# Plain loads in order of need, a first projection by quarters and biases spread by DMA, at the start of a GRU and mixture-of-experts kernel

## The chip, the cores and the metric

The kernel runs on one core of one Trainium2 chip. The metric is the device time of an execution in microseconds; before and after are compared as medians of several runs. Beside the runs there is one profiled execution, from which every duration below is taken.

## The reference

`x` is [8, 256, 512]: 8 sequences of T = 256 steps, the inputs of the GRU; `cond` [8, 512] is its state at the start. A GRU runs over the steps, a mixture of experts with a shared expert follows, and `x` is added.

```python
def cell(h, x):
    gi = x @ W_ih + b_ih          # [512] x [512, 1536]
    gh = h @ W_hh + b_hh
    i_r, i_z, i_n = split(gi, 3); h_r, h_z, h_n = split(gh, 3)
    r = sigmoid(i_r + h_r); z = sigmoid(i_z + h_z)
    n = tanh(i_n + r * h_n)
    h_new = (1 - z) * n + z * h
# over the rows of all h: router, softmax, top 2 of 8 experts, weights normed to 1
out = x + sum_e combine[e] * (silu(g_e) * u_e) @ w_down[e] + (silu(g_s) * u_s) @ w_sh_down
```

All data are float32.

## The kernel before

The time axis is cut into 16 blocks of 16 steps. A block is 8 x 16 = 128 tokens, so one block fills the partitions. For each block the kernel projects `x` with `W_ih` (`project`, TensorE through `multiply`, L310), adds the biases into `gi` (VectorE, L356), and stores `gi` to a DRAM tile (L366 for r and z, L368 for n). From there `load_seeds` (L386) fetches the gate inputs of four steps at a time in the layout of a step, since the tokens' partitions are not those of the step; `turn_seeds` (L391) transposes the n part. A `step` has 48 matmuls (L419) for the gates r, n and z: 16 each, four column groups of the array by four quarters of the state. Before them ScalarE copies the gate inputs into the banks (`open_gate`, L403); afterwards VectorE transposes each bank (L430), and sigmoid, tanh and three more vector operations make the next state (L438 to L455). GpSimd keeps a copy of the states (L458).

Between the steps TensorE is fed with pieces of other work in an order written out by hand: the projections of later blocks, the shared expert (L707), the router. A quota spreads these pieces over the blocks. After the last step come the rest of the shared expert and 35 tiles of routed tokens (L661, L788).

The state's 512 features lie on 128 partitions and 4 quarters q. Before the change feature d = j x 128 + q x 32 + i lies on partition 32 j + i in quarter q. So each weight matrix is loaded by `by_state` in transfers to 32 partitions (L142 for `W_ih`, L152 for `W_hh`, 12 transfers of 256 KB each), and a block of `x` is loaded in 8 transfers to 16 partitions (L119) and transposed in 32 by 32 blocks by VectorE (`transpose_x`, L299). The weights of the GRU lie in the space of the last four experts, which are loaded when the GRU no longer needs it.

The order at the start sets what this text is about. SP issues half of `x_0` (ScalarE's queue the other half and both biases, each to one partition, and the start state), then `W_ih`, `x_1`, `W_hh`, and, from `transpose_x(0)`, `x_2`; only then stand the stores of block 0 and its seed loads. The biases are spread over the partitions by three matmuls with a row of ones (`spread_bias`, L259) and copied by ScalarE (L260), between the third and the fourth quarter of each gate's projection. Before the first step stand `transpose_x(1)` and four pieces of block 1's projection.

The two hardware DMA queues (SP's and ScalarE's) share eight completion semaphores; in the program as built, a transfer first waits until the earlier transfer with the same semaphore has landed.

Of the kernel before, what the change touches and what calls it, by code (L numbers as in the profile page):

```python
# [9 lines left out]
F32 = mybir.dt.float32  # L10
BF16 = mybir.dt.bfloat16
I32 = mybir.dt.int32
AF = mybir.ActivationFunctionType
ALU = mybir.AluOpType
# [3 lines left out]
P = 128  # L18
TS = 16
# [6 lines left out]
def kernel(  # L26
# [48 lines left out]

    nc = tc.nc
    B, T, D = x.shape
    G3 = w_ih.shape[1]  # L80
# [27 lines left out]
    x_tiles = {}  # L108
    NG = 4

    def by_turns(t_, k):

        v = t_.rearrange("(g c) t (j m) -> j c t g m", c=2, j=4)[:, :, k * TS : (k + 1) * TS]
        return [(slice(32 * j + TS * c, 32 * j + TS * (c + 1)), v[j, c]) for j in range(4) for c in range(2)]

    def load_x(k, queues=(nc.sync,)):
        xt = xpool.tile([P, NG, P], F32, tag="x", name=f"x_{k}")
        for i, (ps, src) in enumerate(by_turns(x, k)):
            queues[i % len(queues)].dma_start(xt[ps], src)  # L119
        x_tiles[k] = xt  # L120

    def by_state(w):
# [1 line left out]
        v = w.rearrange("(j q i) n -> j i q n", j=4, i=32)  # L124
        return [(slice(32 * j, 32 * j + 32), v[j]) for j in range(4)]

    load_x(0, (nc.sync, nc.scalar))


    we = wts.tile([P, E, NW, D], F32, name="we")  # L130
    wih = we[:, E - 2 : E].rearrange("p e w n -> p (e w n)").rearrange("p (q n) -> p q n", q=NQ)
    whh = we[:, E - 4 : E - 2].rearrange("p e w n -> p (e w n)").rearrange("p (q n) -> p q n", q=NQ)

    bias = const.tile([P, G3], F32, name="bias")
    bias_row = we[0:1, 0, 0:3].rearrange("p w n -> p (w n)")
    bias_h = we[0:1, 0, 3:5].rearrange("p w n -> p (w n)")
    nc.scalar.dma_start(bias_row, b_ih.unsqueeze(0))
    nc.scalar.dma_start(bias_h, b_hh[0 : 2 * D].unsqueeze(0))
    for g in range(3):
        cols = slice(g * D, (g + 1) * D)  # L140
        for ps, src in by_state(w_ih[:, cols]):
            nc.sync.dma_start(wih[ps, :, cols], src)  # L142
    h = state.tile([P, NQ, 32], F32, name="h")
    nc.vector.memset(h, 0.0)
    h0v = h0.rearrange("b (j q i) -> b j q i", q=NQ, j=4)
    for j in range(4):
        nc.scalar.dma_start(h[32 * j : 32 * j + B], h0v[:, j])
    load_x(1)
    for g in (0, 2, 1):
        cols = slice(g * D, (g + 1) * D)  # L150
        for ps, src in by_state(w_hh[:, cols]):
            nc.sync.dma_start(whh[ps, :, cols], src)  # L152
    wg = wts.tile([P, NQ, 32], F32, name="wg")
    nc.vector.memset(wg, 0.0)
    wsu = [wts.tile([P, NQ, 2, IM], F32, name=f"wsu_{c}") for c in range(NSH)]
# [11 lines left out]
        loads.append(issue)  # L167

    def load_shared():
        load(*((wg[ps, :, 0:E], src) for ps, src in by_state(w_gate)))  # L170
        up = w_sh_gate_up.rearrange("d (two c f) -> two c d f", two=2, f=IM)
        down = w_sh_down.rearrange("(c f p) n -> c p f n", p=P, f=NF)
        for c in range(NSH):
            for two_i in range(2):
                parts = [(wsu[c][ps, :, two_i, :], src) for ps, src in by_state(up[two_i, c])]
                load(*parts[:2])
                load(*parts[2:])
            for f in range(NF):
                load((wsd[c][:, f, :], down[c][:, f, :]))

    def load_expert(e):
        for q in range(NQ):
            load((we[:, e, q, :], w_gate_up[e, q * P : (q + 1) * P, :]))
        for f in range(NF):
            load((we[:, e, NQ + f, :], w_down[e, f * P : (f + 1) * P, :]))


    ident = const.tile([P, P], F32, name="ident")
    make_identity(nc, ident)
    seeds = [const.tile([P, SC, 2 * P], F32, name=f"seeds_{i}") for i in range(NS)]  # L190
    seeds_n = const.tile([P, SC, P], F32, name="seeds_n")
    seed_hn = const.tile([P, P], F32, name="seed_hn")
    states = [const.tile([P, NQ, 32], F32, name=f"hT_{i}") for i in range(NH)]
    for st in [*seeds, seeds_n, seed_hn, *states]:
        nc.vector.memset(st, 0.0)

    tri = const.tile([P, P], BF16, name="tri")
# [51 lines left out]
        ]  # L249
        for i in range(NB)  # L250
    ]
    nc.vector.tensor_tensor(bias_row[:, 0 : 2 * D], bias_row[:, 0 : 2 * D], bias_h, ALU.add)
    one = we[0:1, 2, 0, 0:P]
    nc.vector.memset(one, 1.0)

    def spread_bias(g):
        ps = ps_mm.tile([P, D], F32, tag="mm", name=f"biasp_{g}")
        cols = slice(g * D, (g + 1) * D)
        nc.tensor.matmul(ps, one, bias_row[:, cols], start=True, stop=True)  # L259
        nc.scalar.copy(bias[:, cols], ps)  # L260

    b_hn = b_hh[2 * D : G3].rearrange("(j m) -> j m", j=4)
    for j in range(4):
        nc.gpsimd.dma_start(seed_hn[32 * j : 32 * j + B], b_hn[j].partition_broadcast(B))


    rows = dram.tile([B, T, D], F32, name="rows")
# [5 lines left out]
    nc.vector.tensor_copy(vacant[:, :, 0], lanes)  # L273
    load((listed[0 : E * NM], vacant), (listed[E * NM : E * NM + 1], vacant[0:1]))

    banks = {g: ps_gru.tile([P, D], F32, name=f"ps_{g}") for g in "rnz"}
    for bank in banks.values():  # L280
        nc.tensor.matmul(
            bank[:, 0:P], seeds[0][:, 0, 0:P], seeds[0][:, 0, 0:P], start=True, stop=True
        )


    xT_of = {}

    spare = deque()

# [7 lines left out]
    def transpose_x(k):  # L297
        xT = two.tile([P, NG, NQ, 32], F32, tag="xrT", name=f"xT_{k}")
        nc.vector.transpose(  # L299
            xT.rearrange("p g q s -> p (g q s)"), x_tiles.pop(k).rearrange("p g m -> p (g m)")  # L300
        )
        xT_of[k] = xT
        if k + 2 < NB:
            load_x(k + 2)

    def multiply(ps, lhs, rhs, start, stop):

# [32 lines left out]
    def project(k, g):  # L340

        box = {}

        def issue(q, cols):
            if q == 0 and cols.start == 0:
                box["ps"] = ps_mm.tile([P, D], F32, tag="mm", name=f"gip_{k}_{g}")
            multiply(
                box["ps"][:, cols],
                lambda c: xT_of[k][:, c, q, :],
                wih[:, q, g * D + cols.start : g * D + cols.stop],  # L350
                start=(q == 0 and cols.start == 0),
                stop=(q == NQ - 1 and cols.stop == D),
            )

        def end():
            nc.vector.tensor_tensor(  # L356
                gi[:, :, g, :],
                box["ps"].rearrange("p (j m) -> p j m", j=4),
                bias[:, g * D : (g + 1) * D].rearrange("p (j m) -> p j m", j=4),
                ALU.add,  # L360
            )
            if g > 0:
                to = gi_dram[k][g % 2].rearrange("j b t n -> (b t) j n")
                projected.add((k, "rzn"[g]))
                if g == 1:
                    nc.sync.dma_start(to.rearrange("p j (a n) -> p j a n", a=2), gi[:, :, 0:2, :])  # L366
                else:
                    nc.sync.dma_start(to, gi[:, :, 2, :])  # L368

        return [  # L370
            matmul_piece(lambda cols, q=q: issue(q, cols), end if q == NQ - 1 else None)
            for q in range(NQ)
        ]
# [4 lines left out]
    def load_seeds(c, of="nz"):  # L378

        k, o = divmod(c * SC, TS)  # L380
        steps = slice(o, o + SC)
        for g in of:
            assert (k, g) in projected
            tile_, src = (seeds_n, gi_dram[k][0]) if g == "n" else (seeds[c % NS], gi_dram[k][1])
            for j in range(4):
                nc.sync.dma_start(tile_[32 * j : 32 * j + B], src[j, :, steps, :])  # L386

    def turn_seeds(c):

# [12 lines left out]
        src = {"r": seeds[c % NS][:, t, 0:P], "z": seeds[c % NS][:, t, P : 2 * P], "n": seed_hn}  # L402
        nc.scalar.copy(banks[g][:, 0:P], src[g])  # L403

    whh_v = whh.rearrange("p q (a j m) -> p q a j m", a=3, j=4)
    hc_of = {}

    def hc_of_block(k):
# [2 lines left out]
    def step(n):  # L411
# [3 lines left out]
        for g, bank in banks.items():  # L415
            a = "rzn".index(g)
            for q in range(NQ):
                for j in range(4):
                    nc.tensor.matmul(  # L419
                        bank[32 * j : 32 * j + B, 0:P],  # L420
                        hT[:, q, 0:B],
                        whh_v[:, q, a, j, :],
                        start=False,
                        stop=(q == NQ - 1),
                        skip_group_check=True,
                    )
# [143 lines left out]
    def send_rows(k):  # L570

        hr = two.tile([P, NG, P], F32, tag="y", name=f"hr_{k}")
        nc.vector.transpose(
            hr.rearrange("p g m -> p (g m)"), hc_of_block(k).rearrange("p g q s -> p (g q s)")
        )
        for ps, dst in by_turns(rows, k):
            nc.sync.dma_start(dst, hr[ps])

    laid = {}

# [259 lines left out]
        under_way.update(up=stages, turn=last)  # L840


    transpose_x(0)
    nc.vector.transpose(states[0].rearrange("p q b -> p (q b)"), h.rearrange("p q i -> p (q i)"))
    for g in range(3):
        pieces = project(0, g)
        for piece in pieces[:-1]:
            piece[1]()
        spread_bias(g)
        pieces[-1][1]()  # L850
        if g > 0:
            load_seeds(0, "nzn"[g])
    turn_seeds(0)
    load_seeds(1)
    load_shared()

    projections = deque()
    projections.append((0, lambda: transpose_x(1)))
    for k in range(1, NB):
        for g in range(3):  # L860
            projections.extend(project(k, g))
            if g == 1 and k + 1 < NB:
                projections.append((0, lambda k=k: transpose_x(k + 1)))

    for _ in range(1 + NQ):
        projections.popleft()[1]()
    for g in banks:
        open_gate(0, g)
    for k in range(NB):
# [138 lines left out]
```

## Time and profile before

| | us |
|---|---|
| median of 3 runs | 1495.91 (1495.86 to 1499.71) |
| profiled execution | 1485.87 |
| its span | 1484.1 |
| TensorE matmuls busy | 1411.5 (95%) |
| VectorE busy | 744.3 (50%) |
| ScalarE busy | 418.2 (28%) |
| first projection starts | 11.0 |
| first step's matmuls start | 54.8 |

The page cuts the span into 40 slices of 37.1 us; TensorE's busy share in tenths and the rate of all transfers in the first five slices are 4, 6, 9, 9, 9 and 188, 80, 114, 118, 99 GB/s. In lines of the profile, L followed by a number is a line of the kernel, "<-" leads from an output to its inputs or from a waiting instruction to what ended its wait, SPq and ACTq are the queues of DMA issues of those engines, PE is TensorE, DVE VectorE, ACT ScalarE and POOL GpSimd. A float32 matmul appears as two records on PE.

### The profile page before, as it was taken

To read this page: it belongs to the slowest core of one execution; us is meant where nothing else is said; L and a number is where in the kernel's file an instruction comes from. 1 tells how busy PE (TensorE), PEld (TensorE's weight loads), DVE (VectorE), ACT (ScalarE), POOL (GpSimd) and SP (SyncE) were. 2 spreads that over 40 slices of the span, in tenths; PEclk is the share of its full clock that TensorE was granted. 3 is DMA by queue.
4 is the path that set the end of the run, shared out by engine and by line. 5 is a ranking of instruction groups with operands and counts; after the bars stand their busy time and mean duration, and the time that the engine had idled before them with its cause. 6 is when DMAs were issued, how large, how long until landed. Compare 5 with 4: busy or idle time off the path is not lost.

```text
span 1484.1 us, 75080 instructions
## 1 busy us (share of the span) xinstructions
PE 1411.5 (95%) x33082; PEld 1029.6 (69%) x33082; DVE 744.3 (50%) x2772; ACT 418.2 (28%) x1774; POOL 248.0 (17%) x497
## 2 busy tenths in 40 slices
PE   4699999999999999999999999999999999999995
PEld 1487777777777777877777777787777774444442
DVE  2356555556565556565646565656565643222221
ACT  0133232323333333333333333333333320222221
POOL 1122311111101010100001010101010212344442
PEclk8799999999999999999999999999999999999998
DMA  9244522222312011111011111111011323455453
GB/s 188 80 114 118 99 55 65 59 65 66 71 43 50 15 50 29 36 37 42 17 47 35 30 40 31 29 36 43 14 45 28 94 70 111 86 87 96 88 87 49
DMA packets 69226, 90.68 MB, mean 61 GB/s; under 512 B 13410, under 2 KB 46242, under 8 KB 68900
## 3 DMA queue, kind: packets, MB, share of 16 engines
q1 hardware_dynamic: 53056, 48.14, 12.6%
q0 software_dynamic: 15456, 37.57, 12.5%
q8 instruction: 261, 4.28, 1.2%
q14 instruction: 65, 0.53, 0.1%
q10 hardware_dynamic: 388, 0.16, 0.0%
HBM read 55.50 MB, written 30.32 MB: 58 GB/s over the span
## 4 chain that ended last, share of the span: by engine, by line
PE 90%; DMA 3%; DVE 3%; issue 2%; ACT 1%; SPq 0%; POOL 0%; DVEq 0%; ACTq 0%; POOLq 0%
PE ps_r L419 16%; PE gu_s L707 15%; PE ps_n L419 15%; PE ps_z L419 15%; PE gip L310 9%; PE gu_t L661 8%; PE po L310 7%; PE yp L788 4%; DMA we<-in_L_cond_W_hh_dram 1%; DMA we<-in_L_cond_W_ih_dram 1%; DVE zT L430 1%; DVE hn L454 0%; ACT z L449 0%; DVE hT L455 0%; PE ps_z L768 0%
## 5 line engine op out<-in xcount | busy, mean ns | idle before, releaser
L419 PEld LDWEIGHTS ps_r<-we,hT 128*8 128x8 f32 x8192 | 222.4, 89 | 120.8 <-ACT ps_z L403 72.0
L419 PE MATMUL ps_r<-we,hT 128*8 128x128 f32 x8192 | 278.3, 273 | 17.6 <-DVE hT L455 10.3
L419 PE MATMUL ps_z<-we,hT 128*8 128x128 f32 x8192 | 279.3, 273 | 3.2 <-issue 3.2
L419 PE MATMUL ps_n<-we,hT 128*8 128x128 f32 x8192 | 277.9, 273 | 0.0
L707 PE MATMUL gu_s<-hc,wsu 128*32 128x256 f32 x4096 | 247.2, 379 | 2.1 <-issue 2.1
L458 POOL COPY hc<-hT 128x32 f32<-128x32 f32 x256 | 62.7, 245 | 1045.8 <-DVE hT L455 1045.8
L419 PEld LDWEIGHTS ps_z<-we,hT 128*8 128x8 f32 x8192 | 229.8, 90 | 4.7 <-issue 4.3
L419 PEld LDWEIGHTS ps_n<-we,hT 128*8 128x8 f32 x8192 | 229.8, 90 | 0.2
L310 PE MATMUL gip<-we,xT 128*32 128x512 f32 (+1 forms) x1976 | 197.0, 506 | 29.9 <-DVE xT L299 22.5
L438 ACT ACTIVATE r<-rT 128x32 f32<-128x32 f32 x256 | 58.5, 229 | 508.5 <-DVE rT L430 506.3
L707 PEld LDWEIGHTS gu_s<-hc,wsu 128*32 128x32 f32 x4096 | 140.3, 110 | 84.8 <-issue 16.1
L430 DVE STREAM_TRANSPOSE rT<-ps_r 128x128 f32<-128x128 f32 x256 | 80.3, 314 | 179.3 <-PE ps_r L419 178.5
L430 DVE STREAM_TRANSPOSE nT<-ps_n 128x128 f32<-128x128 f32 x256 | 80.9, 316 | 127.4 <-PE ps_n L419 127.3
L310 PE MATMUL po<-wsd,act_s 128*32 128x256 f32 (+1 forms) x1408 | 134.2, 476 | 0.0
L661 PE MATMUL gu_t<-we,xrT 128*128 x280 | 131.7, 593 | 0.2 <-ACT xrT L770 0.2
L310 PEld LDWEIGHTS gip<-we,xT 128*32 128x32 f32 x1976 | 71.0, 111 | 85.1 <-issue 66.5
L403 ACT COPY ps_n<-seed_hn 128x128 f32<-128x128 f32 x256 | 68.8, 269 | 88.0 <-DVE nT L430 85.6
L430 DVE STREAM_TRANSPOSE zT<-ps_z 128x128 f32<-128x128 f32 x256 | 81.0, 316 | 13.6 <-PE ps_z L419 5.4
L446 ACT ACTIVATE nn<-nt 128x32 f32<-128x32 f32 x256 | 58.8, 230 | 81.6 <-DVE nt L444 81.4
L652 DVE TENSOR_TENSOR act_t<-gu_t,act_t 128x256 f32<-128x256 f32 x35 | 14.9, 424 | 131.4 <-ACT act_t L651 131.4
L794 POOL DMA_INDIRECT out_dram<-y,row x35 | 55.5, 1585 | 113.2 <-DVE y L791 95.9
L403 ACT COPY ps_r<-seeds 128x128 f32<-128x128 f32 x256 | 67.0, 262 | 18.8 <-DMA seeds<-gid_rz 18.6
(162 smaller groups left out, 1146.5 us busy)
## 6 DMA issues: line engine op xcount, KB each, us to landing
gid_rz<-gi SPq DMA_DIRECT2D x16, 512.0 KB
seeds<-gid_rz SPq DMA_DIRECT2D x256, 32.0 KB
we<-in_L_ffn_w_gate_up_dram POOLq DMA_DIRECT2D x32, 256.0 KB, 3.9
gid_n<-gi SPq DMA_DIRECT2D x16, 256.0 KB
seeds_n<-gid_n SPq DMA_DIRECT2D x256, 16.0 KB
wsu<-_L_ffn_w_sh_gate_up_dram POOLq DMA_DIRECT2D x32, 128.0 KB, 3.5
rows<-hr SPq DMA_DIRECT2D x128, 32.0 KB
we<-in_L_ffn_w_down_dram POOLq DMA_DIRECT2D x16, 256.0 KB, 4.0
```

Source lines behind the costliest of these rows:

```text
L310: nc.tensor.matmul(ps[32 * c : 32 * c + 32], lhs(c), rhs, start=start, stop=stop, skip_group_check=True,)
L403: nc.scalar.copy(banks[g][:, 0:P], src[g])
L419: nc.tensor.matmul(bank[32 * j : 32 * j + B, 0:P], hT[:, q, 0:B], whh_v[:, q, a, j, :], start=False, stop=(q == NQ - 1), skip_group_check= ...
L430: nc.vector.transpose(gT.rearrange("p a b -> p (a b)"), banks[g][:, 0:P])
L438: nc.scalar.activation(r, gr, AF.Sigmoid)
L446: nc.scalar.activation(nn, nt, AF.Tanh)
L458: nc.gpsimd.tensor_copy(hc_of_block(k).rearrange("p g q (c t) -> p q g c t", t=TS)[:, :, :, :, t], new.rearrange("p q (g c) -> p q g c", c=2),
L652: nc.vector.tensor_tensor(act, ps[:, 0:IM], act, ALU.mult)
L661: nc.tensor.matmul(box["ps"], lhs(q), w_up(q), start=(q == 0), stop=(q == NQ - 1))
L707: nc.tensor.matmul(box["ps"][32 * g : 32 * g + 32, two_i, :], wsu[c][:, q, two_i, fs], hc_of[m][:, :, q, :], start=(two_i == 0 and q == 0) ...
L788: nc.tensor.matmul(box["y"], lhs, rhs, start=(f == 0), stop=(f == NF - 1))
L794: nc.gpsimd.indirect_dma_start(out=out.rearrange("b t d -> (b t) d"), out_offset=bass.IndirectOffsetOnAxis(ap=laid["row"][:, i : i + 1], a ...
```

## The change

Feature d = q x 128 + 32 j + i now lies on partition 32 j + i in quarter q, so `W_hh` is read with 128 consecutive rows on the partitions: three transfers, one for each gate. For the projection feature d = 4 p + q lies on partition p: a quarter of `W_ih` is one transfer of 128 rows of 6 KB. `x_0` and `x_1` are loaded with a token on each partition, and transposed by TensorE; the later blocks are loaded as before and transposed by VectorE, which reads them with a step of four floats. All these loads stand on SP's queue. The biases are read from DRAM to all 128 partitions, before the last quarter of `W_ih`; `b_hh` for r and z is added on all partitions. The first projection runs over quarters with the gates inside. ScalarE's queue takes the stores of block 0's gate inputs and its seeds, and a warm-up loads the table of the sigmoid. Six pieces of block 1's projection stand before the first step instead of four. Each block of `x` from the fourth on is issued one block later than before. The sums with the biases, the operands of a step, the router's and the shared expert's weights follow the new order of features; the rows of states kept for the experts have the old form with new contents, so that the experts' up weights are now loaded by 32 partitions.

```diff
-    load_x(0, (nc.sync, nc.scalar))
-    nc.scalar.dma_start(bias_row, b_ih.unsqueeze(0))
-    nc.scalar.dma_start(bias_h, b_hh[0 : 2 * D].unsqueeze(0))
-    for g in range(3):
-        cols = slice(g * D, (g + 1) * D)
-        for ps, src in by_state(w_ih[:, cols]):
-            nc.sync.dma_start(wih[ps, :, cols], src)
+    bias_h = we[:, 0, 0:2].rearrange("p w n -> p (w n)")
+    load_x_plain(0)
+    for q in range(NQ):
+        if q == NQ - 1:
+            nc.sync.dma_start(bias, b_ih.partition_broadcast(P))
+            nc.sync.dma_start(bias_h, b_hh[0 : 2 * D].partition_broadcast(P))
+        nc.sync.dma_start(wih[:, q], w_ih.rearrange("(p q) n -> q p n", q=NQ)[q])
+    load_x_plain(1)
+    w_hh_v = w_hh.rearrange("(q p) n -> p q n", p=P)
+    for g in (0, 2, 1):
+        cols = slice(g * D, (g + 1) * D)
+        nc.sync.dma_start(whh[:, :, cols], w_hh_v[:, :, cols])
+    load_x(2)
...
+    nc.scalar.activation(const.tile([P, 1], F32, name="warm"), h[:, 0, B : B + 1], AF.Sigmoid)
...
     def load_expert(e):
-        for q in range(NQ):
-            load((we[:, e, q, :], w_gate_up[e, q * P : (q + 1) * P, :]))
+        for ps, src in by_state(w_gate_up[e]):
+            load((we[ps, e, 0:NQ, :], src))
...
+    def load_x_plain(k):
+        xt = xpool.tile([P, D], F32, tag="x", name=f"x_{k}")
+        nc.sync.dma_start(xt, x[:, k * TS : (k + 1) * TS, :])
+        x_tiles[k] = xt
...
+    def turn_x_plain(k):
+        ps = ps_o.tile([P, NQ, P], F32, tag="po", name=f"xTp_{k}")
+        xt = x_tiles.pop(k)
+        for q in range(NQ):
+            nc.tensor.transpose(ps[:, q, :], xt.rearrange("p (m q) -> p q m", q=NQ)[:, q], ident)
+        xT_of[k] = two.tile([P, NG, NQ, 32], F32, tag="xrT", name=f"xT_{k}")
+        nc.vector.tensor_copy(
+            xT_of[k].rearrange("p g q s -> p q g s"), ps.rearrange("p q (g s) -> p q g s", g=NG)
+        )
...
     def transpose_x(k):
         xT = two.tile([P, NG, NQ, 32], F32, tag="xrT", name=f"xT_{k}")
         nc.vector.transpose(
-            xT.rearrange("p g q s -> p (g q s)"), x_tiles.pop(k).rearrange("p g m -> p (g m)")
+            xT.rearrange("p g q s -> p (g q s)"), x_tiles.pop(k).rearrange("p g (i q) -> p g q i", q=NQ)
         )
-        if k + 2 < NB:
-            load_x(k + 2)
+        if k + 1 < NB:
+            load_x(k + 1)
...
+                by = nc.sync if k else nc.scalar
-                    nc.sync.dma_start(to.rearrange("p j (a n) -> p j a n", a=2), gi[:, :, 0:2, :])
+                    by.dma_start(to.rearrange("p j (a n) -> p j a n", a=2), gi[:, :, 0:2, :])
-                nc.sync.dma_start(tile_[32 * j : 32 * j + B], src[j, :, steps, :])
+                by = nc.sync if c else nc.scalar
+                by.dma_start(tile_[32 * j : 32 * j + B], src[j, :, steps, :])
...
-    whh_v = whh.rearrange("p q (a j m) -> p q a j m", a=3, j=4)
+    whh_v = whh.rearrange("p q (a k j i) -> p q a j k i", a=3, k=NQ, j=4)
...
-    transpose_x(0)
     nc.vector.transpose(states[0].rearrange("p q b -> p (q b)"), h.rearrange("p q i -> p (q i)"))
-    for g in range(3):
-        pieces = project(0, g)
-        for piece in pieces[:-1]:
-            piece[1]()
-        spread_bias(g)
-        pieces[-1][1]()
-        if g > 0:
-            load_seeds(0, "nzn"[g])
-    turn_seeds(0)
-    load_seeds(1)
+    nc.vector.tensor_tensor(bias[:, 0 : 2 * D], bias[:, 0 : 2 * D], bias_h, ALU.add)
+    first = [project(0, g) for g in range(3)]
+    for q in range(NQ):
+        for g in range(3):
+            first[g][q][1]()
+    load_seeds(0, "z")
+    load_seeds(0, "n")
...
-    for _ in range(1 + NQ):
+    turn_x_plain(1)
+    for _ in range(NQ + NQ // 2):
         projections.popleft()[1]()
+    turn_seeds(0)
+    load_seeds(1)
```

## The prediction

> **What bounds the kernel now.** I read the page first: PE is busy 95% of the span, slices 2 to 39 of 40 are full, and only the first (37.1 us) shows 4 tenths. So TensorE is the bound after the start, and at the start it is something else. The chain that ended last, in order of time, says what (columns: start us, us, what):
>
> ```profile
> 11.23 9.28 DMA we<-in_L_cond_W_ih_dram
> ...
> 22.30 6.50 DMA we<-in_L_cond_W_hh_dram
> ...
> 28.82 9.69 DMA we<-in_L_cond_W_hh_dram
> 38.51 0.02 issue
> 38.53 0.31 SPq L119
> ...
> 38.96 2.87 DMA gid_rz<-gi
> ...
> 46.62 1.58 DMA seeds_n<-gid_n
> ...
> 49.77 5.24 PE gip L310 x32
> 55.02 0.87 PE ps_r L419 x32
> 55.89 0.87 PE ps_n L419 x32
> 56.76 0.87 PE ps_z L419 x32
> ```
>
> The first step's three gates run from 55.02 to 57.64. Before them stand the weights, landed at 38.51, then the trip of the gate inputs to DRAM and back (38.96 to 48.2), then a projection at half pace. From the list of waits, SP's first, then PE's:
>
> ```profile
> SPq L119 <- DMA we<-in_L_cond_W_hh_dram: 7.1, 8, 0.9
> SPq L119 <- DMA we<-in_L_cond_W_ih_dram: 6.6, 8, 1.0
> ```
> ```profile
> PE gip L310 <- DVE xT L299: 22.5, 1, 22.5
> ```
>
> The sums that the first store needs are ready at 23.5 (timeline: L356 at 22.80, 0.69 long), but the store stands behind W_hh and eight x loads on SP, and each of those loads waits for a W_hh transfer. The built order shows why: the two hardware queues share eight completion semaphores in rotation, and a transfer waits for the earlier owner of its semaphore. So the store leaves 15 us late, and PE idles 22.5 us. The table of stages gives the pace of loading (last columns: granted clock, DMA share, GB/s):
>
> ```profile
> 4.00:27.00 23.00, 15.99 (x102) 4.03 (x102) 5.14 (x22) 3.04 (x4) 2.61 (x5) 1.00 0.94 197
> 28.00:38.00 10.00, 0.00 (x0) 0.00 (x0) 0.11 (x1) 0.00 (x0) 0.00 (x0) 0.56 1.02 201
> 1239.20:1241.40 2.20, 2.20 (x48) 1.34 (x44) 0.00 (x0) 0.00 (x0) 0.00 (x0) 1.00 0.98 385
> ```
>
> Loads to 32 partitions move about 200 GB/s with the engines full; loads of 2 KB rows to 128 partitions (x again, experts' rows, in the third line) move 385 at the same share. The second line also shows the clock falling while PE is idle.
>
> **The change, part by part.**
>
> *Bytes and pace.* W_ih and W_hh are 3.15 MB each, a block of x 0.26 MB. New are the spread biases: 128 x 6 KB and 128 x 4 KB, 1.31 MB, where 10 KB were loaded. Up to the last quarter of W_ih the queue carries 0.26 + 3.15 + 1.31 = 4.72 MB. I take 360 GB/s for the plain loads, a little below the 385 row since starts and short gaps are in it. The broadcast has no row: 3.4 us at 385, 6.6 at the 200 of the first rows, and no sure upper end (a rival below). I take 5. First data moves at 2.0. Then x_0 and three quarters, 2.62 MB: 7.3 us, to 9.3. Biases: 14.3. Last quarter 2.2: 16.5, some 17 with the completion (27 us stood here before, PE included).
>
> *First projection by quarters.* 48 matmuls of 512 columns as before, but gates r, z, n per quarter. Two records each: 24 records took 4.99 us at first and 32 took 3.64 once warm. Quarter 0 arrives at 5 and takes 5 us, quarters 1 and 2 end by 16, quarter 3 runs 17 to 19.8. The three bias spreads on PE (1.1 us each) and the ACT copies go. The sums in DVE (0.69 each, the bias add of 1.2 already done) end for z at 19.7, for n at 20.5. Their operands now come in runs of 32 elements; I charge nothing, and 0.7 more each would be the dearest.
>
> *Four transposes of x_0 and x_1 on PE*, one read every fourth float, and a DVE copy: they wait for x alone, before quarter 0 and between projections, where PE has room.
>
> *Stores and seeds of block 0 on ACT.* The store of r and z is issued at 19.8, past SP's waits. ACT's earlier work, four h0 loads and the sigmoid table with its warm-up, ends by about 6, so nothing waits behind it. The rule that speaks against: the Trainium skill, DMA: Bandwidth & Descriptors, section Issuing engines are not separate DMA queues, says that a second queue saves issue time only, since all run on the same 16 engines. By the row gid_rz takes 2.87 us (alone), landing at 22.7; sharing half of each engine with W_hh it takes 5.7, landing at 25.5. I take the rule's, but it decides nothing: in the new program the third seed transfer takes the semaphore of W_hh's z part and must wait for it anyway. What counts is that 0.79 MB of stores delay the weights, 2 us.
>
> *W_hh.* After 16.5: x_1 0.7, W_hh 8.7, stores 2.0, so the end is 28 and the completion 29 (38.5 before). Then the new chain: third seed issue 0.3, landing 1.6 (the seeds_n row above), the third seeds_n transfer, which waits for it, 0.3, the fourth 0.3, landing 1.6: 33.1; its transpose 0.7. ACT opens the gates when it has issued these, near 31.7, and PE starts the step at 32. x_2's loads now stand behind W_hh and land about 30; they are needed only after the second step.
>
> *The step itself.* PE has been idle since about 27 (six pieces of projection 1, 24 matmuls, 5.5 us after 21), so its clock will be near one half, as in the 28 to 38 row. r, n and z then take 1.75 us each, to 37.2, against 57.64: **20.4 us**. At full clock it would be 23.
>
> *Work moved ahead of the first step:* 24 matmuls of projection 1 where 16 stood, 8 fewer later, where PE is the bound: 8 x 0.227 = **1.8 us**, of which some may return as waits, so 1.6.
>
> *Every later block.* The W_hh operand is read in 4 runs of 32 columns. The row for it is the shared units', which read the hidden states in runs of 32 as well: 64 records in 3.45 us is 0.211 ns a column, against 0.213 for the step now. Cost nothing. x_2 to x_15 (14 blocks) are transposed by DVE with one float per 16 bytes. The trace has 0.67 to 0.70 us for the contiguous form. A rule speaks against: the Trainium skill, SBUF — State Buffer, Door 1: The DMA port swizzle, notes that SBUF works in 16-byte lines, of which at least two accesses should use each. By the row the sum is unchanged; by the rule, taken as a doubling (an estimate), DVE gets 14 x 0.7 = 9.8 us, at most half of it in the way of a step. I take 0.5. Loads of x run one block ahead, not two: 22 us early against a landing of 3. The first MoE weights go to 128 partitions, the experts' up weights to 32 at about 200 GB/s: 1.3 us each instead of 0.7, covered by the shared units, which last until 1263; the late experts' loads are issued by 1236.
>
> Sum: 20.4 + 1.6 - 0.5 = 21.5, about **22 us**. Profiled execution: 1485.87 (span 1484.1 and 1.8 around it), so 1464. The median of the runs is 10.0 above that execution; I take the same saving from it: 1495.9 - 22 = **1474**.
>
> **Rivals.**
> 1. *The loads stay at 200 GB/s*, because the pace belongs to HBM or to full engines (share 1.02 at 201). 8.92 MB, stores included, take 44.6 us, the weights land at 47, the step starts at 50 and ends at 55 cold: 2.4 + 1.6 gives 4, so 1492. Against it stands the 385 row; it was short, though.
> 2. *The broadcast reads the same 10 KB 128 times and is served slowly.* This is the case of the other side. One engine's pace in the 385 row is 24 GB/s; were the common row served at that pace, 1.31 MB take 55 us, 50 more than charged, so 28 us slower: 1524. It decides from 27 us, at 49 GB/s. Nothing in the trace measures it; the b_hh spread by POOL (8 copies) lands in 4.7 us but is 4 KB a piece. At 100 GB/s, 13 us, there is still a gain of 14 (1482).
> 3. *Strided reads slow the steps.* 256 steps at 2.62 us are 671 us, and 3.3% eats the whole gain. Against it is the shared units' row. DVE's strided transposes at their dearest cost 5: 1479.
> 4. *No effect*, that the first step was bound by something later: excluded by the chain, where no compute but 5.24 us of projection stands between weights and step.
>
> **How the numbers follow.** The sum above: 0.72, with its own range 1469 to 1480 (loads at 385 with biases at 3.4 give the step at 29, 25 us; loads at 300 give 32.7 for the weights, 18 us). Rival 1: 0.09. Rival 2: 0.10, of which 0.05 beyond the deciding point. Rival 3: 0.08, of which 0.03 slower. Nothing: 0.01. A range of 1467 to 1488 leaves out part of rival 1 and the far ends. A change under 0.3% (4.5 us) is about what a measurement can't tell. Faster: 0.72 + 0.04 + 0.05 + 0.05 = 0.86; same 0.06; slower 0.08.
>
> **What would show it.** Loads at 330 to 385 GB/s between 3 and 28 us; last quarter of W_ih landed near 17; gid_rz issued by ACT near 20; PE's first step gates starting near 32 with a clock of about a half; the interval from there to the end shorter by 1 to 2 us; step matmuls unchanged at 0.87 us for 32. A bias transfer longer than 10 us, or a first step after 45, would make the prediction wrong.

## The result, and the profile after

| | before | after |
|---|---|---|
| median, us | 1495.95 (1495.86 to 1499.71) | 1481.91 (1477.91 to 1482.67) |
| profiled execution | 1485.87 | 1481.67 |
| its span | 1484.1 | 1479.9 |
| first step's matmuls start | 54.83 | 33.62 |
| second step's matmuls start | 59.16 | 40.08 |
| last step's matmuls start | 1212.29 | 1207.41 |

The change is a gain: 14.0 us by the medians, where 22 were forecast. The ratio on record is 0.9884 [0.9867, 0.9900], which would be 17.3 us (15 to 20), so this first comparison leaves some 3 us open. The two profiled executions differ by 4.2 us only, because the one of before lay 10 us under its median. So something of the start's gain is missing, in the medians a little and in the traces much.

The chain that ended last of the kernel after, in order of time (start us, us, what):

```profile
...
7.62 9.63 DMA we<-in_L_cond_W_ih_dram
...
17.29 1.97 PE gip L320 x16
...
20.00 8.60 DMA gid_rz<-gi
...
28.62 1.93 DMA x<-in_x_dram
...
30.57 2.72 DMA seeds_n<-gid_n
...
33.62 1.89 PE ps_r L434 x32
35.51 1.71 PE ps_n L434 x32
37.22 1.32 PE ps_z L434 x32
...
40.25 0.87 PE ps_r L434 x32
```

The two waits for `W_hh`, 16 us of the chain before, are gone from it. The store of r and z leaves at 20.00, not at 38.96; it takes 8.60 us instead of 2.87. The three gates of the first step take 4.9 us instead of 2.6: the clock is cold. The r gate of the second step runs at the old pace, 0.87 for 32 records.

The table of stages (stretch, its length, busy us of PE, its weight loads, DVE, ACT and POOL with their instructions, granted clock, DMA share, GB/s):

```profile
3.00:17.00 14.00, 11.06 (x81) 3.72 (x79) 5.44 (x22) 1.49 (x2) 3.13 (x10) 1.00 1.01 361
17.00:28.00 11.00, 9.04 (x80) 2.69 (x76) 2.72 (x4) 0.00 (x0) 0.00 (x0) 1.00 1.03 340
34.00:38.00 4.00, 4.00 (x83) 2.98 (x76) 1.54 (x4) 0.66 (x3) 0.00 (x0) 0.50 0.15 34
```

The loads move 361 and 340 GB/s with the engines full, where 197 and 201 stood. The third line is the first step at a clock of 0.50.

The list of PE's waits (what waited, for what; us in total, times, longest):

```profile
PE ps_r L434 <- DVE hT L470: 13.3, 28, 0.8
PE ps_r L434 <- ACT ps_r L418: 6.7, 1, 6.7
PE ps_z L434 <- issue: 5.2, 7, 1.2
```

The waits of 22.5 and 7.1 us ahead of the projections of blocks 1 and 0 are gone; 6.7 ahead of the first step have come. But two lines that belong to the steps have grown: PE waiting for a new state has 13.3 where before (L455 there) it had 10.3, and idle time in front of the z gate for which nothing is shown has 5.2 where it had 3.2.

Where the span went in these two executions, by stretch: up to the second step's start 19.1 us were gained (59.16 - 40.08); from there to the last step 14.2 were lost (1167.33 against 1153.13); after it the same within 0.7. What the 14.2 are shows in one line of the table of stages for that stretch, first of before, then of after:

```profile
59.16:1212.29 1153.13, 1129.95 (x31401) 895.21 (x31394) 658.42 (x2562) 360.48 (x1640) 142.44 (x372) 1.00 0.20 51
```
```profile
40.08:1207.41 1167.33, 1137.58 (x31417) 911.92 (x31410) 662.90 (x2562) 359.37 (x1640) 134.36 (x353) 1.00 0.20 50
```

PE is busy 7.6 us longer with nearly the same instructions, at the same granted clock, and idle 6.6 us longer (29.75 against 23.18). The experiments have to say whether either belongs to the change.

### The profile page after: what moved, and what is told of

Its sections match the earlier page's. It is cut to its first block, busy times and chain, and to the rows that moved or that the text cites. A ratio compares the mean times of both kernels' runs of the same rounds, so it can differ in the third digit from the quotient of the medians.

```text
span 1479.9 us, 75070 instructions
## 1 busy us (share of the span) xinstructions
PE 1419.9 (96%) x33116; PEld 1050.2 (71%) x33116; DVE 748.9 (51%) x2771; ACT 414.1 (28%) x1771; POOL 240.4 (16%) x478
## 4 chain that ended last, share of the span: by engine, by line
PE 91%; DVE 3%; issue 2%; DMA 2%; ACT 1%; POOL 0%; DVEq 0%; SPq 0%; ACTq 0%; POOLq 0%
PE ps_r L434 16%; PE ps_n L434 15%; PE gu_s L723 15%; PE ps_z L434 15%; PE gip L320 9%; PE gu_t L677 8%; PE po L320 7%; PE yp L804 4%; DMA we<-in_L_cond_W_ih_dram 1%; DVE zT L445 1%; DMA gid_rz<-gi 1%; DVE hn L469 0%; DVE hT L470 0%; ACT z L464 0%; PE ps_z L784 0%
## 5 line engine op out<-in xcount | busy, mean ns | idle before, releaser
L434 PE MATMUL ps_r<-we,hT 128*8 128x128 f32 x8192 | 278.8, 273 | 26.7 <-DVE hT L470 13.3
L434 PE MATMUL ps_n<-we,hT 128*8 128x128 f32 x8192 | 287.1, 273 | 2.2 <-issue 1.5
L434 PE MATMUL ps_z<-we,hT 128*8 128x128 f32 x8192 | 283.1, 273 | 5.4 <-issue 5.2
L723 PEld LDWEIGHTS gu_s<-hc,wsu 128*32 128x32 f32 x4096 | 155.6, 110 | 71.6 <-issue 14.3
L320 PE MATMUL gip<-we,xT 128*32 128x512 f32 (+1 forms) x1976 | 192.0, 501 | 2.7 <-DVE xT L217 1.6
L320 PE MATMUL po<-wsd,act_s 128*32 128x256 f32 (+1 forms) x1440 | 137.6, 469 | 0.0
L320 PEld LDWEIGHTS gip<-we,xT 128*32 128x32 f32 x1976 | 67.9, 111 | 57.2 <-issue 42.6
L668 DVE TENSOR_TENSOR act_s<-gu_s,act_s 128x256 f32<-128x256 f32 x64 | 27.1, 424 | 91.8 <-ACT act_s L667 86.2
```

The costliest lines, as they stand in the source:

```text
L320: nc.tensor.matmul(ps[32 * c : 32 * c + 32], lhs(c), rhs, start=start, stop=stop, skip_group_check=True,)
L434: nc.tensor.matmul(bank[32 * j : 32 * j + B, 0:P].rearrange("b (k i) -> b k i", k=NQ), hT[:, q, 0:B], whh_v[:, q, a, j, :], start=False, s ...
L668: nc.vector.tensor_tensor(act, ps[:, 0:IM], act, ALU.mult)
L723: nc.tensor.matmul(box["ps"][32 * g : 32 * g + 32, two_i, :], wsu[c][:, q, two_i, fs], hc_of[m][:, :, q, :], start=(two_i == 0 and q == 0) ...
```

## The experiments

Every ratio below is against the kernel before on the same chip. The start of a step is read from the trace as the first record of its r gate.

### Both kernels again, on two further chips

b_again and b_third are the kernel before, a_again and a_third the kernel after, unedited.

> The kernel before, unchanged, for its trace on the chip of the other runs: the profiled execution of before (1485.9 us) lies 10 us below the four timed ones. If that execution was a lucky one, this one takes 1494 to 1497 us and the surplus is found as TensorE idle with no releaser in steps 14 to 42. If the chip makes the difference, both its time and the timed runs are near 1486.

> The changed kernel, unchanged, on the same chip. Theory 1 (start gains 19 us, later blocks lose some 5 us to the slower transposes): ratio 0.988 to 0.991. Theory 2 (the loss after the start is chance in instruction fetches and not the change's): ratio 0.984 to 0.988.

> The kernel before, unchanged, for a trace on the chip of the three runs beside it. Theory (what follows the second step's start varies with the chip and with where TensorE's instruction fetches fall): steps 1 to 255 take 1153 to 1160 us here.

> The changed kernel, unchanged. Theory (the start gives 21 us up to the second step, the stretch from there to the last step returns some 3): second step starts at 39 to 40.5, steps 1 to 255 take 0 to 6 us longer than those of before in the trace from the same chip, block 15 has 1.5 us or more of TensorE idle inside steps. Rival (the stretch returns nothing but for chance): as long or shorter than before's.

| | b_again | a_again | b_third | a_third |
|---|---|---|---|---|
| median, us | 1493.80 | 1476.44 | 1490.23 | 1471.19 |
| ratio | 1.0000 | 0.9883 [0.9864, 0.9903] | 0.9994 | 0.9863 [0.9843, 0.9883] |
| second step starts | 60.89 | 39.53 | 59.76 | 40.16 |
| second to last step | 1159.40 | 1163.23 | 1154.06 | 1158.57 |
| of it PE busy | 1136.88 | 1136.23 | 1130.10 | 1129.88 |
| of it PE idle | 22.52 | 27.00 | 23.96 | 28.69 |
| idle for a new state | 11.1 | 13.4 | 10.9 | 13.9 |
| idle for `place` | 2.9 | 1.0 | 2.8 | 1.0 |
| idle, nothing shown | 3.5 | 6.8 | 5.6 | 8.9 |

The lines for the stretch from the second to the last step, b_third and then a_third:

```profile
59.76:1213.82 1154.06, 1130.10 (x31401) 900.92 (x31393) 659.21 (x2562) 360.51 (x1640) 142.26 (x372) 1.00 0.20 51
```
```profile
40.16:1198.74 1158.58, 1129.88 (x31417) 905.37 (x31409) 664.24 (x2562) 360.04 (x1640) 134.30 (x353) 1.00 0.20 51
```

And PE's waits in that stretch, in the same order:

```profile
PE ps_r L419 <- DVE hT L455: 10.9, 26, 0.8
PE ps_z L419 <- issue: 4.6, 4, 2.2
PE ps_r L419 <- DVE place L539: 2.8, 4, 1.3
```
```profile
PE ps_r L434 <- DVE hT L470: 13.9, 28, 0.8
PE ps_z L434 <- issue: 5.2, 5, 2.7
PE ps_n L434 <- issue: 3.3, 2, 1.8
PE ps_r L434 <- DVE place L554: 1.0, 2, 0.5
```

Three things follow. First, the busy time goes with the chip or the execution, not with the kernel: on one chip it agrees within 0.7 us between the kernels, and between the chips it differs by 6 to 7. The first profile of before has 1130 and the one of after 1138, which is more than half of the 14.2 lost there. It is not a slower pace of every step. Measured from start to start, fourteen of the sixteen positions in a block have medians that agree within 0.005 us between b_again and b_third; the seventh and the eighth step take 5.37 and 4.50 in b_again, 5.21 and 4.18 in b_third. Summed over blocks 1 to 15, these two positions take 146.6 to 149.4 us in all four traces of b_again's chip and in the first one of after, and 139.8 to 141.9 in the nine others, the first one of before among them. What holds them up isn't shown.

Second, up to the second step 21.4 and 19.6 us are gained, as forecast; the first to the second step takes 6.0 and 7.0 in these two traces of the kernel after, so part of the difference is when the clock came back (at 37.0 and 38.7).

Third, in these pairs of traces 3.8 and 4.5 us are given back in the steps, and they are idle time of PE: by the lines that have a name, a new state comes 2.3 and 3.0 us later in sum, gaps with nothing shown add 3.3 and 3.3, and the waits for `place` (the router's work) give 1.9 and 1.8 back. The medians say less: the same-chip pairs gain 17.8 and 19.9 us (1494.19 - 1476.44 and 1491.08 - 1471.19), so 3.6 of the start's gain is missing in the first pair and nothing in the second, where the traced execution of b_third was the quickest of its twelve.

Two things came otherwise than expected: the surplus of b_again over the first profile is busy time, not idle time in a few blocks, and a_third shows no gap in the middle of block 15's steps, where a_again has 2.0 us. The ratios of a_again and a_third don't part the two theories that stood for a_again.

The gaps with nothing shown have a mark, which the expectations guessed at when they spoke of instruction fetches. The page has a DMA queue named instruction, here of a_third (packets, MB, share of the engines):

```profile
q8 instruction: 262, 4.29, 1.3%
```

Its packets are 16 KB each. Taking the stretch from the second to the last step in all fourteen traces of this case, 104 of the 130 gaps over 0.15 us with nothing shown (77 of 90 us) end 1.15 to 1.70 us after such a packet has ended; of all moments 12% lie so, and of the gaps that have a name 22%. So PE most likely waits there for its next instructions. Why they come late in these places, and more often in one kernel than in another, isn't shown.

### Do the slower transposes cost the steps their time?

The transposes of VectorE that read every fourth float are slower, as the lines of after and of a_contig show (minimum, median, maximum in ns):

```profile
L309 DVE STREAM_TRANSPOSE xT<-x x14: 1115/1137/1146, 40.9 to 997.6; 128x512 f32<-128x512 f32 x14
```
```profile
L309 DVE STREAM_TRANSPOSE xT<-x x14: 692/702/706, 39.7 to 994.2; 128x512 f32<-128x512 f32 x14
```

a_contig takes the strided reading away from the kernel after; b_strided puts it into the kernel before.

```diff
 a_contig
-            ... x_tiles.pop(k).rearrange("p g (i q) -> p g q i", q=NQ)
+            ... x_tiles.pop(k).rearrange("p g m -> p (g m)")
 b_strided
-            ... x_tiles.pop(k).rearrange("p g m -> p (g m)")
+            ... x_tiles.pop(k).rearrange("p g m -> p (g m)" if k < 2 else "p g (i q) -> p g q i", ...)
```

> The changed kernel with VectorE's transposes of x_2 to x_15 reading contiguous columns as before; the features then stand in another order than W_ih's rows, so the projections from block 2 on are not the reference's. Theory 1 (14 transposes of 1.14 us instead of 0.70 delay two steps of each block by 0.2 us): 4 to 6 us faster than the changed kernel, and the second half of the gap of 0.2 us in the two steps of each block is gone. Rival (the lengthening is hidden in VectorE's slack, the loss is in instruction fetches): within 1 us of the changed kernel.

> The kernel before with the strided read in the transposes of x_2 to x_15 alone; the projections from block 2 on are not the reference's. Theory 1: 4 to 6 us slower than before (ratio 1.003 to 1.004), transposes of 1.14 us. Rival: no difference.

a_contig: 1476.88, ratio 0.988 [0.986, 0.9899], against 1476.44 for a_again on the same chip. The features of the later blocks stand in another order there, but the part after the last step has 35 tiles as before, so the totals can be compared. The transposes save 14 x 0.435 = 6.1 us of VectorE and nothing of the time that the medians show; PE's waits for a new state between the second and the last step fall by 1.5 (13.4 to 11.9). So the theory that asked for 4 to 6 us from the length of the transposes falls; a cost of 1 or 2 can't be told from none by these runs.

b_strided: 1531.71, ratio 1.0253 [1.0234, 1.0272], but this total says nothing of transposes. With features in another order the states are others, and the router sends the tokens elsewhere, so that the part after the last step has 39 tiles, as the scaling of the experts' products shows (b_again: x35):

```profile
L792 DVE TENSOR_SCALAR y<-yp,share 128x512 f32<-128x512 f32 x39 | 29.3, 751 | 19.4 <-PE yp L789 19.4
```

That part takes 307.0 us instead of 272.4. From the second to the last step b_strided is 3.1 us over b_again (1162.48 against 1159.40), 0.3 of it in PE's busy time and 0.7 in waits for a new state. So in the kernel before the longer transposes may have cost up to 3, in the kernel after no total shows a cost; neither is the 4 to 6.

### The order alone

b_act is the kernel before with nothing but the stores and seeds of block 0 on ScalarE's queue; all loads, their shapes and their pace stay.

```diff
+                by = nc.sync if k else nc.scalar
-                    nc.sync.dma_start(to.rearrange("p j (a n) -> p j a n", a=2), gi[:, :, 0:2, :])
+                    by.dma_start(to.rearrange("p j (a n) -> p j a n", a=2), gi[:, :, 0:2, :])
...
-                nc.sync.dma_start(tile_[32 * j : 32 * j + B], src[j, :, steps, :])
+                (nc.sync if c else nc.scalar).dma_start(tile_[32 * j : 32 * j + B], src[j, :, steps, :])
```

> The kernel before with the stores and seeds of block 0 on ScalarE's queue alone. Theory (the store stands 15 us in SP's queue before; W_hh at 200 GB/s still lands near 39 to 41): gid_rz is issued near 24, the first step starts at 46 to 49, 7 to 10 us are gained. Rival (a store that shares the engines with W_hh and seeds that wait for semaphores of the loads take as long as they stood in the queue): start after 52, under 4 us gained.

1479.91, ratio 0.9926 [0.9907, 0.9946]: 10.5 us by the medians, more than half of the 17.8 and 19.9 that the whole change gains on two other chips. From its chain:

```profile
23.67 2.81 DMA gid_rz<-gi
...
32.80 3.94 DMA seeds_n<-gid_n
...
38.32 5.91 PE gip L310 x32
44.23 0.87 PE ps_r L420 x32
```

The store leaves as soon as its sums are there (before: 38.96), and the first step starts at 44.0, 2 us earlier than the early end of what was expected. The second projection, 32 records, still takes 5.9 us, most of it at a clock of 0.50, after a wait of 10.9 for its transposed block. So leaving SP's queue is worth some 10 us by itself, and the pace of the loads, the quarters, the transposes on PE and the rest together the next 7 to 9 (17.8 and 19.9 less 10.5, across chips).

### The biases

a_nospread loads one row of each bias to one partition in place of all 128 (1.31 MB are left out).

```diff
+    nc.gpsimd.memset(bias, 0.0)
+    nc.gpsimd.memset(bias_h, 0.0)
...
-            nc.sync.dma_start(bias, b_ih.partition_broadcast(P))
-            nc.sync.dma_start(bias_h, b_hh[0 : 2 * D].partition_broadcast(P))
+            nc.sync.dma_start(bias[0:1], b_ih.unsqueeze(0))
+            nc.sync.dma_start(bias_h[0:1], b_hh[0 : 2 * D].unsqueeze(0))
```

> The changed kernel with one row of each bias loaded and GpSimd setting the other rows to zero, so that 1.31 MB of broadcast are left out (the biases are missing on 127 partitions and the states are others; the routing and the end of the kernel may change with it, so only the start is read). Theory (the broadcast runs at the full rate of some 390 GB/s): the last quarter of W_ih lands 3.4 us earlier (near 13.9) and the first step starts 3 to 3.5 us earlier, near 30. Rival (the broadcast of one row is slow): more than 5 us earlier. Rival (the start does not hang on it): no earlier.

The total, 1504.06, isn't read: here too the routing is another, with 39 tiles. The start can be read, from the chain:

```profile
...
7.77 12.00 PE gip L322 x96
...
31.99 1.90 PE ps_r L436 x32
```

The first step starts 1.4 us earlier than in a_oldexp of the same chip, whose start is that of the kernel after (33.40), not the 3 to 3.5 that the bytes would give. The reason is in the first line: once `x_0` has landed and is turned, the first projection runs 12.0 us without a gap, so PE alone sets its end. With the biases the last quarter of `W_ih` landed at 17.24 in the kernel after, when PE had been done with the third for 0.06 us: the two limits meet, and what is saved on the queue gains little here. Up to the second step 2.6 us are gained (37.6 against 40.2), but that depends on when the clock comes back: the first to the second step takes 5.6 here and 5.8 to 7.1 in the seven traces that start as the kernel after does. That the spread runs at full pace shows in the kernel after. The 128 rows of 4 KB of `b_hh` are on their way from 11.94 to 14.43 by the trace's packets, so the second stretch holds the spread, and the first the plain loads before it:

```profile
6.00:10.00 4.00, 3.13 (x16) 1.33 (x20) 2.56 (x7) 0.00 (x0) 1.63 (x3) 1.00 1.01 402
10.00:14.00 4.00, 4.00 (x36) 1.04 (x32) 1.65 (x15) 1.49 (x2) 1.14 (x3) 1.00 1.02 395
```

### W_hh to 32 partitions again

```diff
-        nc.sync.dma_start(whh[:, :, cols], w_hh_v[:, :, cols])
+        for j in range(4):
+            ps = slice(32 * j, 32 * j + 32)
+            nc.sync.dma_start(whh[ps, :, cols], w_hh_v[ps, :, cols])
```

> The changed kernel with each W_hh transfer cut into four of 32 partitions. Theory (32 partitions move 200 GB/s, 128 move near 390): W_hh takes 7 to 8 us longer, the first step starts at 39 to 42, and the time is 6 to 8 us above the changed kernel's. Rival (all that matters is the order in the queue, and the stores share the engines anyway): start within 2 us of 33.5.

1474.16, ratio 0.9893 [0.987, 0.9916]. The r gate isn't late (31.9), but the others wait, as its chain and its line for 34 to 38 us show:

```profile
32.39 5.99 DMA we<-in_L_cond_W_hh_dram
...
39.72 1.90 PE ps_z L436 x32
```
```profile
34.00:38.00 4.00, 1.90 (x32) 1.15 (x32) 0.99 (x4) 0.89 (x4) 0.00 (x0) 0.50 1.07 219
```

With full engines (share 1.07) the loads move 219 GB/s, and 197 from 17 to 28 us (share 0.90), where the kernel after has 340. The second step starts at 44.79, against 40.16 in a_oldexp, which starts as the kernel after does and ran on this chip: the pace of `W_hh` is worth 4.6 us at the start. The medians differ by 6.2.

### The experts' loads

Since a_again idled 2.0 us in the middle of block 15's steps, near the loads of the experts' up weights, a_oldexp has these loaded to 128 partitions by quarters, as before. a_oldexp2 is the same kernel on the chip of a_third. Both leave out that the experts' rows follow the new order, so their routed sums are not the reference's; the routing is.

```diff
-        for ps, src in by_state(w_gate_up[e]):
-            load((we[ps, e, 0:NQ, :], src))
+        for q in range(NQ):
+            load((we[:, e, q, :], w_gate_up[e, q * P : (q + 1) * P, :]))
```

> The changed kernel with the experts' up weights loaded as before, by quarters to 128 partitions; their rows then don't match the order of the features, so the routed experts' sums are not the reference's. Theory 3 (transfers to 32 partitions hold TensorE's instruction fetches back): TensorE's idle time inside steps falls from 2.0 to under 0.5 us in block 15 and from 1.7 to under 1.0 us in block 2, and steps 246 to 250 are 2 us shorter in sum; time 3 us less. Rival (the stalls come from where the fetches fall in the program, which any edit moves): block 15 keeps 1.4 to 2.4 us of them.

> The changed kernel with the experts' up weights loaded to 128 partitions again (rows not in the order of the features, so the routed sums are not the reference's; the routing is). Theory 3 (32-partition loads hold instruction fetches back): block 15's idle time inside steps under 0.3 us while the unchanged one beside it has 1.5 or more; 2 to 4 us less in all. Rival (chip or phase): both have it, or neither.

a_oldexp: 1467.99, ratio 0.9846 [0.9816, 0.9875], and no gap in block 15. That seemed to fit, but a_hh32 and a_nospread, which keep the new loads, have no gap there either. The pair on one chip decides: a_oldexp2 at 1471.25 (0.987 [0.9851, 0.9889]) and a_third at 1471.19, neither with a gap in block 15. The shape of these loads costs nothing that can be seen.

These kernels say one thing more. On the chip of b_act, which keeps everything behind the start as in the kernel before, b_act takes 1157.7 us from the second to the last step, a_oldexp 1153.1 and a_hh32 1152.2. So the new form isn't slower in the steps on every chip and in every build.

### The transpose to another place

a_apart is the kernel after with the transposes of the blocks from the third on issued later: after the second piece of gate n's projection, not between gates z and n.

```diff
         for g in range(3):
-            projections.extend(project(k, g))
-            if g == 1 and k + 1 < NB:
-                projections.append((0, lambda k=k: transpose_x(k + 1)))
+            pieces = project(k, g)
+            if g == 2 and k + 1 < NB:
+                pieces.insert(2, (0, lambda k=k: transpose_x(k + 1)))
+            projections.extend(pieces)
```

> The changed kernel with each strided transpose of x moved two pieces of projection later, away from the sum with the bias that VectorE does just before it. Theory 1, what is left of it (1.14 us behind 0.69 holds the next step's transposes up): the steps where the pair stood get shorter by 0.2 to 0.4 us each, 2 to 5 us less in all. Rival (hidden in slack, as the contiguous form's run of no gain says): within 1.5 us.

1466.66, ratio 0.9839 [0.9819, 0.9859], the quickest of the versions that leave nothing out. By means it is 3.9 us below a_third on the same chip, with a standard error of 1.2 worked out from the 5 and 4 runs. PE's waits in the stretch from the second to the last step:

```profile
PE ps_r L434 <- DVE hT L470: 10.7, 24, 0.8
PE ps_n L434 <- issue: 1.8, 2, 1.6
PE ps_z L434 <- issue: 1.5, 3, 0.5
```

The waits for a new state are back at before's (10.7 against 10.9; a_third has 13.9). They are 10.1 to 11.1 in the three traces of the kernel before and in that of b_act, and 12.7 to 13.9 in the seven traces that have the long transposes in their first place (after, a_again, a_third, a_oldexp, a_oldexp2, a_hh32, a_nospread). So this part can be ascribed to the transposes, by their place; the idle time with nothing shown, 5.5 instead of 8.9, can't.

## Why the prediction was right, and which term of it was mis-sized

The median lies inside the range of 1467 to 1488, on the side that was forecast, 7.9 us above the number and 1.9 above the likeliest case's own range. Point by point:

*Bytes and pace: right.* 361 GB/s against 360; the last quarter of `W_ih` landed at 17.24 against 17. The rival of loads at 200 GB/s is excluded: that pace belongs to the form with 32 partitions, as a_hh32 shows on the same bytes.

*The biases: right, and cheaper than they looked.* 5 us were charged; they move at 395 GB/s, so 1.31 MB take 3.3 us, near the early end of the bounds. The rival of the other side, a slow service of one common row, is excluded.

*The first projection: right in its end, and in part by luck.* Quarter 0 was to start at 5, and PE to be done by 16 and wait for quarter 3's weights until 17. `x_0` landed only after 5.4 to 5.9 us, its transposes and copy took two more, and from 7.97 to 20.07 PE worked with a single pause of 0.06. That PE reached quarter 3 just as its weights came is chance; the end came at 20 all the same. In the forecast's view less to load would have helped by what it saved; a_nospread saved 3.3 us of transfers and the first step came 1.4 earlier.

*The store of r and z: its rule was right and its size too small.* The row said 2.87, the Trainium skill's page DMA: Bandwidth & Descriptors (section Issuing engines are not separate DMA queues) that the engines are shared, from which 5.7 was estimated. It took 8.6. It was to decide nothing, because the third seed transfer would wait for `W_hh` anyway; in the chain the store, ending at 28.6, is what the first seeds follow. The forecast also had `x_2`'s loads out of the way. In the chain one of them takes over the store's semaphore (28.62, 1.93 long), and a transfer of the n part's seeds waits for it until 30.57. Since `W_hh` was due at 29, the start of the step moved little: 33.1 to 33.7 in the traces of the kernel after, a_apart and a_oldexp2, not 32.

The opposite use of that section is what the experiments correct. As a reason against a second queue it would have said that b_act saves issue time only, 0.27 to 0.41 us for each transfer by the issues on ScalarE's queue in the trace of after. b_act measured 10.5 us: what a queue free of other waits is worth depends on those waits, here 15 us of the store's delay.

*The cold clock: right.* 0.50 granted in the first step, 4.9 us for its gates against 5.2.

*The first step as a whole: right.* 20.4 us forecast; up to the second step 21.4 and 19.6 on one chip, 19.1 in the first two profiles.

*Every later block and the work moved ahead: this is the term that was mis-sized.* The forecast has 1.6 gained and 0.5 lost after the first step, 1.1 in all, and said that this stretch would become 1 to 2 us shorter. In the traces of the pairs on one chip it became 3.8 and 4.5 us longer, an error of about 5; by the medians 3.6 and nothing. Of its parts:
- *Work moved ahead.* The 16 records of projections fewer are in the trace, but PE's busy time fell by 0.7 and 0.2, not 1.8. In the same stretch 16 matmuls more of the shared expert's second product were issued in halves (records of 256 columns x832 instead of x768, of 512 x608 instead of x640); that these ate the rest was not measured apart.
- *Slower transposes.* 1.14 us against 0.70, a factor of 1.63, between the row and the doubling estimated from the Trainium skill's page SBUF — State Buffer, section Door 1: The DMA port swizzle. Without their length a_contig has 1.5 us less of waits for a new state and no time that its total could show: the 0.5 was not far off, but the place where the transposes stand was not weighed.
- *What no step of the prediction had.* The blocks were costed by the length of instructions; the gaps between them were not. PE's waits for a new state grew by 2.3 and 3.0 us, and a_apart, which only puts the transposes elsewhere among the pieces, takes that back. The waits for `place` became 1.9 and 1.8 shorter, unforeseen too. These two, 0.4 and 1.2 us together, are all that can be put down to the change. Idle time for which the trace names nothing grew by 3.3 in both pairs. It is 5.5 in a_apart, 5.8 in a_oldexp2 and 8.7 in b_act, so it goes up and down with edits that have nothing to do with it, the small one of b_act included. Most of it follows packets of instructions; what makes these late stays open.
- *Strided operands in the steps and in the sums: right at nothing.* 32 records still take 0.87 us, and the sums with the bias a median of 0.68 in both.

*The conversion to the median* took the saving of the sum over unchanged. That is no small matter here: the profile of before is of an execution with PE busy for 1130 us in the steps, and others have 1137. By the medians the change gains 14.0, 17.8 and 19.9 us on three occasions; with the term above as the traces have it, 20.4 - 4.2 = 16 lies among them. Why the first of the three is the smallest isn't settled: its ratio would make it 17.3, and its two profiles differ in the seventh and eighth steps of a block.

## What to carry to other kernels

Ask first whether a store that everything waits for stands behind loads that wait for each other: here a small edit that gave it and the seeds behind it another queue brought 10.5 us, more than the 7 to 9 of everything else in the change. Then give loads 128 partitions, 340 to 361 GB/s instead of about 200. When a gain of some 20 us is looked for in traces of 1480, take both on one chip and split each stretch into busy and idle, and the idle time by what ended it: here the busy part went with the chip, the gaps with nothing shown went with the build, and only the waits with a name showed what the change had done.

## What was not expected of the hardware

- A row of 4 or 6 KB read from DRAM to all 128 partitions moves at 395 GB/s, nearly as quick as the plain loads before it (402).
- A store of 512 KB that takes 2.8 to 2.9 us alone took 8.6 beside a bulk load, more than an equal share of the engines (5.7) would give.
- PE's busy time from the second to the last step was 1130 or 1137 us, by the chip or execution, at a granted clock of 1.00 in the rows: 0.6%, twice the 0.3% that the prediction took as the least that can be told. The difference sits in two of the sixteen steps of a block (146.6 to 149.4 us in sum against 139.8 to 141.9).
- Of 130 gaps of PE with nothing shown, 104 end 1.15 to 1.70 us after a 16 KB packet of the instruction queue.
- A transpose of 128 x 512 floats on VectorE takes 1.14 us with one float in four read, 0.70 with all in order.
